# A cross-attention kernel with prompt tokens: first inner products in chunks, loads by order of use, last key chunk computed with the values

## The chip, the cores and the metric

The kernel runs on one core of a Trainium2 chip. The metric is the device time of one execution in microseconds. A core has TensorE (PE; its weight loads are shown as PEld), VectorE (DVE), ScalarE (ACT), GpSimd (POOL) and SyncE (SP, which here only issues transfers). Each engine runs its own instructions in order and waits for the others by semaphores; transfers (DMA) are issued by an engine and run beside it.

## What is computed

Eight batches (B). In each, 112 rows of x (S) attend with 20 heads of 16 channels (C = 320) to 371 text tokens and 4 prompt tokens, all rows of `ctx` (375 x 512). Everything is float32. Cut to what matters:

```python
q   = heads(x @ W_q)
k_t = heads(text @ W_k);  v_t = heads(text @ W_v)
probs_t  = softmax(q k_t^T / 4)
text_out = probs_t v_t
qsem = l2norm(probs_t @ text)              # 512 wide, per head and row
sem  = qsem @ l2norm(ip)^T                 # 4 numbers per head and row
fused = q k_ip^T / 4 + 0.5 * sem
ip_out = (softmax(fused) * spatial_mask) v_ip
out = (text_out + ip_out) @ W_out + b_out + x
```

The kernel never forms `qsem`. Its norm and its products with the prompts come from inner products of the context rows with each other: with G = ctx ctx^T, the squared norm of `p @ text` is p G p^T, and the products with the prompts are p times the last columns of G. G is symmetric, so only its upper triangle is computed, off-diagonal parts doubled ("first inner products" in the title are G for batch 0).

## The kernel before, in words

**For each batch** the context is loaded (`load_ctx`), transposed on TensorE (`transposed_context`, L339) into `ctxT` (512 channels as 4 chunks of 128 partitions, by tokens), and three products are made from it, each in three chunks of four matmuls (over the 4 channel chunks):

- `gram` (L362): G in three row chunks of 128 tokens, with 375, 247 and 119 columns. ACT doubles each out of PSUM into `ug` (L370), POOL halves the diagonal blocks (L371). `gram_to_dram` writes `ug` to a DRAM buffer `ud`, and `gram_to_groups` reads it back (L383) into `u`, once for each of four bands of 32 partitions, with token index modulo 32 on the partition.
- `values` (L409): 320 columns, in three token chunks, copied by ACT into `vext` (L416), written to DRAM (`vd`, L420) and read back by bands into `vr` (L429). `placed` (L445, POOL) copies the 16 value columns of the heads at hand from `vr` into the end of each region of `u`.
- `keys` (L393): the channels in chunks of 128, 371 token columns each. The third chunk has only 64 real columns (320 = 2 x 128 + 64), which `spread` has put apart with zeros between, so that each head lies in its band of 32 partitions. ACT copies each to `kT` (L400).

**The main loop** goes over batches and, in each, five groups of four heads (`steps`). `multiplied(b, g)` (L523) runs 48 products of 32-token blocks of probabilities with `u`: one pass gives p G, the text output, the softmax sum and the prompt products. In it, the scores (L476) and probabilities (L489 on DVE, L493 on ACT) of the step two ahead are made; SP carries the probabilities to `xg` (L496) and DVE transposes them in blocks (L504). `reduced` then takes the four PSUM banks of the step (ACT L536, DVE L538).

**The work for the next batch** is placed after the steps of the batch at hand, by `between`: after group 0 the inner products, after group 1 two chunks of values, after group 2 the third chunk of values and the first of keys, after group 3 the other two of keys, after group 4 the transposed context of the batch after it, and, in batches 1, 3 and 5, the queries of the next pair of batches (`project_queries`, L281 to L301). `finish` (softmax over prompts, sums, output projection) of the batch before is placed there too: its transposes (L620) after group 3, its output product (L633) after group 4, and the copy that empties that bank (L640).

**The order** of instructions on TensorE, SP and DVE is the order of the program text (a manual schedule), and of ACT and POOL too until the main loop. SP's transfers share eight semaphores in turn: each issue waits until the transfer eight before it has landed. So the order in which SP issues, and what an issue waits for, decides what stands behind it. ACT's queue issues a few transfers of the beginning.

PSUM has eight banks: four for `qd` (`ps_qd`), two for scores (`ps_sc`), two for everything else (`ps_mm`). `bank(name)` takes one of the last, `bank(name, spare=True)` one of the scores'.

**The beginning** (L700 to L742), before the loop: prompts normalised, context 0 transposed, its inner products, values, queries, keys, with the first scores between the key chunks; then context 1, the prompt projections (L237), and the first `placed`. SP's order there: context 0, W_v, W_k, the three writes of `ud`, W_k_ip, context 1, the twelve loads of `u`, the four of `vr`, then the probabilities of the first two steps. ACT's: the prompt rows, x of batch 0, W_q, and later `vd`.

## Time and profile before

| | us |
|---|---|
| median of 3 runs (497.8 to 499.25) | 498.68 |
| the profiled execution | 498.01 |
| its span, from first to last instruction | 496.2 |
| main loop starts (first L523) | 44.20 |
| last batch starts (first L523 of batch 7) | 437.13 |
| keys L393, 24 instructions of a batch (batches 1 to 7) | 7.67 |
| values L409, 24 instructions of a batch | 6.85 |
| inner products L362, 24 instructions: batch 0, and a later batch | 7.91, 5.27 |
| DMA: 61075 packets, 67.24 MB, mean rate | 136 GB/s |

One page shows one execution. Busy times are by engine; "the chain" is the work that ended last, followed back from the end, so a piece of work in it has its length in the time. Rows of the timeline give start, duration, engine, line, operation, tiles and sizes, and in brackets how long the engine had been idle and what ended that. `PE` matmuls overlap, so a row's own duration is longer than its share of the chain.

### The profile page before, as it was taken

The page shows a single profiled execution, that of the slowest core. Times are in us where ns is not written, and L with a number is a line of the kernel's source. Part 1 is how long each engine was busy: PE and PEld are TensorE (multiplying, and loading weights), DVE is VectorE, ACT ScalarE, POOL GpSimd, SP SyncE. Part 2 cuts the span into 40 slices and gives each one's busy share as a digit, 9 for nine tenths or more (in the row PEclk, how much of TensorE's full clock was granted, in tenths as well). Part 3 has the DMA queues.
Part 4 walks back from the last instruction along what each step waited for, and adds up shares of the span by engine and source line. Part 5 has one row for each costly group of instructions (what it writes and reads, how often), then busy time and mean ns, then how long its engine had stood idle before and what let it go on. Part 6 is the DMA issues. An engine that isn't in the chain of part 4 may idle for free.

```text
span 496.2 us, 12853 instructions
## 1 busy us (share of the span) xinstructions
PE 468.3 (94%) x5106; PEld 361.8 (73%) x5106; DVE 321.1 (65%) x692; ACT 180.1 (36%) x505; POOL 105.9 (21%) x245
## 2 busy tenths in 40 slices
PE   6999999999999999999999999999999999987963
PEld 3657777788777787788778787788777887766751
DVE  3045456687765775687756776687756776678862
ACT  2253232235334352335324342335324432243232
POOL 4301200002501124012501124012501232011540
PEclk9997999999999999999999999999999999998895
DMA  7588447542595236942595236842595227732300
GB/s 217 157 198 237 100 152 163 156 114 63 154 228 153 58 95 172 210 121 67 163 229 142 67 98 171 199 116 76 171 220 140 67 87 162 195 101 78 101 13 12
DMA packets 61075, 67.24 MB, mean 136 GB/s; under 512 B 22128, under 2 KB 56192, under 8 KB 61016
## 3 DMA queue, kind: packets, MB, share of 16 engines
q1 hardware_dynamic: 60096, 65.32, 50.3%
q10 hardware_dynamic: 920, 1.11, 0.8%
q8 instruction: 40, 0.66, 0.6%
q14 instruction: 19, 0.16, 0.1%
HBM read 31.65 MB, written 8.17 MB: 80 GB/s over the span
## 4 chain that ended last, share of the span: by engine, by line
PE 84%; DVE 5%; ACT 3%; DMA 2%; POOL 2%; issue 2%; SPq 1%; POOLq 0%; ACTq 0%; DVEq 0%
PE ps_qd L523 37%; PE ps_k L393 11%; PE ps_v L409 11%; PE ps_g L362 9%; PE ps_s L476 7%; PE ps_q L289 2%; PE ps_c L339 2%; PE ps_o L633 2%; DVE junk L538 1%; POOL wv L606 1%; DMA vr<-vd 1%; DVE qm L298 1%; PE ps_kip L237 1%; PE ps_ip L456 1%; DMA ip_sb<-in_ctx_dram 1%
## 5 line engine op out<-in xcount | busy, mean ns | idle before, releaser
L523 PE MATMUL ps_qd<-u,xgT 32*112 32x296 f32 (+11 forms) x3840 | 244.4, 365 | 3.5 <-POOL u L445 1.4
L523 PEld LDWEIGHTS ps_qd<-u,xgT 32*112 32x112 f32 x3840 | 196.8, 174 | 33.6 <-issue 7.3
L493 ACT ACTIVATE p<-ps_s,nmx 112x371 f32<-112x371 f32 x160 | 82.3, 568 | 159.8 <-DVE nmx L489 141.6
L489 DVE TENSOR_REDUCE nmx<-ps_s 112x1 f32<-112x371 f32 x160 | 77.4, 528 | 76.0 <-PE ps_s L476 74.7
L504 DVE STREAM_TRANSPOSE xgT<-xg 128x1536 f32<-128x1536 f32 x40 | 118.9, 2971 | 5.2 <-DMA xg<-p 5.2
L538 DVE CUSTOM_DVE_ANT_0 junk<-ps_qd,p 112x371 f32<-112x371 f32 x160 | 87.1, 544 | 45.3 <-ACT pvs L536 28.0
L476 PE MATMUL ps_s<-kT,qm 32*112 32x371 f32 x320 | 75.0, 496 | 2.8 <-ACT p L493 2.2
L445 POOL COPY u<-vr 128x64 f32<-128x64 f32 x120 | 26.6, 238 | 224.8 <-PE ps_qd L523 161.5
L393 PE MATMUL ps_k<-ctxT,wk_sb 128*128 128x371 f32 x192 | 63.6, 480 | 0.0
L409 PE MATMUL ps_v<-wv_sb,ctxT 128*128 128x320 f32 x192 | 55.6, 440 | 0.0
L393 PEld LDWEIGHTS ps_k<-ctxT,wk_sb 128*128 128x128 f32 x192 | 35.7, 190 | 21.7 <-issue 1.1
L476 PEld LDWEIGHTS ps_s<-kT,qm 32*112 32x112 f32 x320 | 36.8, 173 | 15.8 <-ACT kT L400 3.2
L362 PE MATMUL ps_g<-ctxT 128*128 128x375 f32 (+2 forms) x192 | 45.3, 394 | 0.7 <-issue 0.7
L409 PEld LDWEIGHTS ps_v<-wv_sb,ctxT 128*128 128x128 f32 x192 | 35.2, 190 | 13.5
L362 PEld LDWEIGHTS ps_g<-ctxT 128*128 128x128 f32 x192 | 33.4, 197 | 12.3 <-issue 3.8
L400 ACT COPY kT<-ps_k 128x371 f32<-128x371 f32 x24 | 11.3, 469 | 41.4 <-PE ps_k L393 41.3
L606 POOL TENSOR_TENSOR wv<-vip,w 112x1280 f32<-112x1280 f32 (+1 forms) x8 | 19.2, 2404 | 31.8 <-DVE w L604 31.8
L298 DVE TENSOR_SCALAR qm<-ps_q,emask 128x224 f32<-128x224 f32 (+1 forms) x25 | 9.2, 400 | 24.2 <-PE ps_q L289 24.0
L416 ACT COPY vext<-ps_v 128x320 f32<-128x320 f32 x24 | 10.2, 427 | 33.5 <-PE ps_v L409 33.5
L371 POOL TENSOR_TENSOR ug<-ug,half 128x128 f32<-128x128 f32 (+1 forms) x24 | 11.3, 472 | 41.6 <-ACT ug L370 41.6
L536 ACT COPY pvs<-ps_qd 112x21 f32<-112x21 f32 x160 | 16.5, 200 | 6.9 <-PE ps_qd L523 6.9
L289 PE MATMUL ps_q<-xT,wq_sb 128*128 128x224 f32 (+1 forms) x90 | 16.8, 332 | 1.9 <-ACT xT L284 0.9
(95 smaller groups left out, 272.4 us busy)
## 6 DMA issues: line engine op xcount, KB each, us to landing
xg<-p SPq DMA_DIRECT2D x160, 162.3 KB
u<-ud SPq DMA_DIRECT2D x32, 188.0 KB
vip<-vipd SPq DMA_DIRECT2D x8, 560.0 KB
ct<-in_ctx_dram SPq DMA_DIRECT2D x16, 256.0 KB
u<-ud SPq DMA_DIRECT2D x32, 124.0 KB
vr<-vd SPq DMA_DIRECT2D x32, 120.0 KB
vd<-vext SPq DMA_DIRECT2D x7, 480.0 KB
ud<-ug SPq DMA_DIRECT2D x7, 372.0 KB
```

Of the source, the lines that this page charges most:

```text
L289: nc.tensor.matmul(ps[:, : n * S], wq_sb[:, j, i * P : (i + 1) * P], xT[:, j, : n * S], start=(j == 0), stop=(j == NC - 1),)
L362: nc.tensor.matmul(ps[:, : T - t0], ctxT[:, e, t0 : t0 + P], ctxT[:, e, t0:T], start=(e == 0), stop=(e == NE - 1),)
L393: nc.tensor.matmul(ps[:, :TT], wk_sb[:, e, i * P : (i + 1) * P], s["ctxT"][:, e, :TT], start=(e == 0), stop=(e == NE - 1),)
L409: nc.tensor.matmul(ps[:, :C], ctxT[:, e, c * P : (c + 1) * P], wv_sb[:, e, :], start=(e == 0), stop=(e == NE - 1),)
L445: nc.gpsimd.tensor_copy(region(b, c)[:, :, UV - c * P :], s["vr"][:, c * QN : (c + 1) * QN, g, :])
L476: nc.tensor.matmul(ps[:S, :TT], qm[a * RG : (a + 1) * RG, i, r, j * S : (j + 1) * S], s["kT"][a * RG : (a + 1) * RG, i, :], start=True, st ...
L489: nc.vector.tensor_reduce(nmx, ps[:S, :TT], AX.X, ALU.max, negate=True)
L493: nc.scalar.activation(p, ps[:S, :TT], AF.Exp, bias=nmx)
L504: nc.vector.transpose(xT.rearrange("p j (k q) -> p q j k", q=QN), xg.rearrange("p q (j k) -> p q j k", k=RG),)
L523: nc.tensor.matmul(banks[a][:S, j * RG : UW], xT[a * RG : (a + 1) * RG, j, :S], region(b, c)[a * RG : (a + 1) * RG, q, q * RG :], start=(j ...
L538: nc.vector.tensor_tensor_reduce(out=junk, in0=ps[:S, :TT], in1=s["p", g][:, a, :], scale=1.0, scalar=0.0, op0=ALU.mult, op1=ALU.add, accu ...
L606: eng.tensor_tensor(wv, s["vip"][:, :, part], w.rearrange("p h n -> p n h").unsqueeze(3).to_broadcast([S, NIP, n, D]), ALU.mult,)
```

## The change

Five things, in the order of the diff. (1) The inner products of batch 0 are computed by column chunks: when token chunk c of the context is transposed, the blocks (r, c) with r up to c are multiplied, into three banks kept open (`first_gram`); 24 matmuls of 128 (or 119) columns stand in place of 12 of 375, 247 and 119. Between the pieces stand the transposes of the prompts. `awake(n)` issues n matmuls of the identity with itself into a spare bank that nobody reads, eight before the first context transposes and four after them. (2) `ud` becomes three DRAM buffers with rows as `u` holds them, value columns included (zeros), so that a band is read back by 32 rows of 1568, 1056 or 544 numbers each instead of 128 shorter ones; the writes are three per batch instead of one. (3) In batches 1 to 7 the third key chunk isn't computed by itself: its 64 columns of W_k are appended to W_v, the value matmuls have 384 columns, POOL copies the key columns into `k3` (token by spread channel, with zeros that are set once), and three transposes bring them into `kT`. (4) x and W_q move from ACT's queue to SP's, between W_v and W_k; in the beginning the loads of `u` and `vr` stand ahead of context 1 and W_k_ip. (5) The small tiles of `finish` have one buffer instead of two, and the bank of its transposes is one of the scores' in batches 0 to 6.

```diff
+    wv_sb = const.tile([P, NE, C + REST], F32, tag="wv_sb", name="wv_sb")
...
-    nc.scalar.dma_start(x_sb[:, 0, :], x[0])
-    load_channels(nc.scalar, wq_sb, w_q)
...
     load_embed(nc.sync, wv_in, w_v)
+    nc.sync.dma_start(x_sb[:, 0, :], x[0])
+    load_channels(nc.sync, wq_sb, w_q)
     load_embed(nc.sync, wk_sb, w_k)
...
+        s["ud"] = [dram.tile([RG, QN, WC[c]], F32, tag=f"ud{c}", name=f"ud_{b}_{c}") for c in range(NT)]
+        s["vext"] = work.tile([P, NT, C + REST], F32, tag="vext", name=f"vext_{b}", bufs=1)
...
+    def awake(n):
+        ps = bank(f"ps_w_{n}", spare=True)
+        for _ in range(n):
+            nc.tensor.matmul(ps[:, :P], ident, ident, start=True, stop=True)
+
+    def first_gram():
+        ctxT = st[0]["ctxT"]
+        banks = []
+        for c in range(NT):
+            banks.append(ps_qd.tile([P, 512], F32, tag="qd", name=f"ps_g_0_{c}"))
+            if c == NT - 1:
+                nc.gpsimd.tensor_copy(ctxT[:, :, TT:T], ipnT[:, :, :NIP])
+            c0, c1 = c * P, min(c * P + P, T)
+            for r in range(c + 1):
+                for e in range(NE):
+                    nc.tensor.matmul(
+                        banks[r][:, c0 - r * P : c1 - r * P],
+                        ctxT[:, e, r * P : (r + 1) * P],
+                        ctxT[:, e, c0:c1],
+                        start=(e == 0), stop=(e == NE - 1),
+                    )
+            yield
+        for c in range(NT):
+            doubled(banks[c], c)
+            yield
...
     def gram_to_dram(b, c0=0, c1=NT):
-        cols = slice(GCOL[c0], GCOL[c1])
-        nc.sync.dma_start(st[b]["ud"][:, cols], ug[:, cols])
+        for c in range(c0, c1):
+            nc.sync.dma_start(
+                st[b]["ud"][c].rearrange("i q w -> q i w"), ug[:, GCOL[c] : GCOL[c + 1]]
+            )
...
-                    region(b, c)[a * RG : (a + 1) * RG, :, : UV - c * P],
-                    s["ud"][:, GCOL[c] : GCOL[c + 1]].rearrange("(q i) t -> i q t", i=RG),
+                    s["u"][a * RG : (a + 1) * RG, OFF[c] : OFF[c] + QN * WC[c]],
+                    s["ud"][c].rearrange("i q w -> i (q w)"),
...
+            if b > 0 and i == FULL:
+                for c in range(NT):
+                    rows = min(P, TT - c * P)
+                    nc.tensor.transpose(
+                        ps[:, c * P : c * P + rows],
+                        s["k3"][:rows, c].rearrange("p a r d -> p (a r d)"),
+                        ident[:rows, :rows],
+                    )
+                nc.scalar.copy(s["kT"][:, i, :], ps[:, :TT])
+                yield
+                return
...
+        w = C if b == 0 else C + REST
...
+            if b > 0 and c == NT - 1:
+                nc.gpsimd.tensor_copy(
+                    s["k3"][:, :, :, 0, :],
+                    vext[:, :, C:].rearrange("p c (a d) -> p c a d", d=D),
+                )
...
-        ps = bank(f"ps_a_{b}_{h0}")
+        ps = bank(f"ps_a_{b}_{h0}", spare=b < B - 1)
...
     prompts = normalised_prompts()
     context = transposed_context(0)
-    products = gram(0)
+    products = first_gram()
+    next(prompts)
+    awake(8)
+    next(context)
+    awake(4)
+    next(context)
+    next(products)
     next(prompts)
     next(context)
-    next(context)
-    next(prompts)
-    next(context)
+    next(products)
+    next(products)
     order_values()
     for c in range(NT):
         next(products)
         gram_to_dram(0, c, c + 1)
     drain(values(0))
+    gram_to_groups(0, range(NT))
     values_to_dram(0, nc.scalar)
+    values_to_groups(0, nc.sync)
+    loaded[1] = load_ctx(1)
     load_embed(nc.sync, wkip_sb, w_k_ip)
     spread(nc.gpsimd, wq_sb)
+    nc.gpsimd.tensor_copy(wv_sb[:, :, C:], wk_sb[:, :, FULL * P : C])
     spread(nc.gpsimd, wk_sb)
     drain(project_queries(pairs[0]))
-    loaded[1] = load_ctx(1)
     run(("k", 0), lambda: keys(0))
-    gram_to_groups(0, range(NT))
-    values_to_groups(0, nc.sync)
```

`doubled` is the doubling and halving that stood in `gram` (L369 to L371).

## The prediction

> **What bounds the kernel now.** I read the page first (busy shares and the chain that ended last), then the chain in order of time for one batch, then the timeline of the first 45 us and of the places where one batch passes to the next, then the DMA packet records there.
>
> ```profile
> PE 468.3 (94%) x5106; PEld 361.8 (73%) x5106; DVE 321.1 (65%) x692; ACT 180.1 (36%) x505; POOL 105.9 (21%) x245
> ...
> PE 84%; DVE 5%; ACT 3%; DMA 2%; POOL 2%; issue 2%; SPq 1%; POOLq 0%; ACTq 0%; DVEq 0%
> ```
>
> The chain in order of time (start, us, what), one batch:
>
> ```profile
> 123.24 4.50 PE ps_v L409 x16
> 134.11 2.35 PE ps_v L409 x8
> 144.81 5.18 PE ps_k L393 x16
> 156.14 1.42 PE ps_c L339 x12
> ```
>
> TensorE is the bound in the steady part: it is busy 94% and carries 84% of the chain, and the projections of the next batch (values L409, keys L393) stand in the chain with their whole length. Time taken off them there is time off the end, as long as nothing else becomes late. A float32 matmul shows as two instructions, so x8 is one chunk of four matmuls.
>
> The beginning, first in busy times by stretch (TensorE with its number of instructions first, the granted clock third from the end), then in the timeline:
>
> ```profile
> 13.00:14.00 1.00, 1.00 (x3) 0.66 (x2) 0.00 (x0) 0.00 (x0) 0.00 (x0) 1.00 0.00 0
> 15.00:16.00 1.00, 1.00 (x6) 0.93 (x5) 0.00 (x0) 0.03 (x1) 0.46 (x1) 1.00 0.00 0
> ```
>
> ```profile
> 9.17 7.91 PE L362 MATMUL ps_g<-ctxT 128*128 128x375 f32 x24 [0.68 <-issue]
> ...
> 35.15 7.29 SPq L496 DMA_DIRECT2D xg<-p  x8
> ...
> 41.20 2.91 DVE L504 STREAM_TRANSPOSE xgT<-xg 128x1536 f32<-128x1536 f32 x1 [3.97 <-DMA xg<-p]
> ...
> 44.20 1.65 PE L523 MATMUL ps_qd<-u,xgT 32*112 32x392 f32 x6 [0.79 <-issue]
> ```
>
> The first inner products L362 take 7.91 us here and 5.27 us in each later batch. Weight loads of the 375-wide ones are 0.625 us apart until 14.3 us, though the clock column says 1.00: 375 columns in half of that would be the later pace, so TensorE ran at half speed until about 14.2 us, some 5.0 us after these matmuls began. From 9.17 to 43.4 us TensorE has work nearly throughout. The main loop then starts at 44.2 us, when L504 has ended, and L504 waited for the probabilities' transfer, issued only at 35.15 because SP was still at the loads before it.
>
> The timeline where batch 0 passes to 1, 1 to 2, 2 to 3 and 6 to 7:
>
> ```profile
> 103.60 0.59 POOL L445 COPY u<-vr 128x64 f32<-128x64 f32 x3 [6.12 <-DMA vr<-vd]
> ...
> 158.38 0.59 POOL L445 COPY u<-vr 128x64 f32<-128x64 f32 x3 [8.05 <-DMA vr<-vd]
> ...
> 215.53 0.59 POOL L445 COPY u<-vr 128x64 f32<-128x64 f32 x3 [7.32 <-DMA vr<-vd]
> 217.59 0.48 DVE L640 TENSOR_TENSOR ob<-ps_o,xb 112x320 f32<-112x320 f32 x1
> ...
> 436.84 0.59 POOL L445 COPY u<-vr 128x64 f32<-128x64 f32 x3 [13.32 <-DMA vr<-vd]
> 437.13 1.66 PE L523 MATMUL ps_qd<-u,xgT 32*112 32x392 f32 x7 [0.25 <-POOL u L445]
> ```
>
> At each change of batch the values of the next one come back through DRAM (vd, then vr) and POOL places them (L445) just before TensorE needs them. This is the second limit.
>
> **Keys behind the values (7 of 8 batches).** Removed: the third key chunk, 8 instructions at 5.18/16 = 0.324 us, 2.59 us. Added: 24 value instructions of 384 columns instead of 320. One of 320 costs (4.50+2.35)/24 = 0.285 us, one of 371 (keys) 0.324; by proportion 384 costs 0.335 to 0.342, so 0.050 to 0.057 more, 24 of them 1.2 to 1.4; I take 1.28. Three transposes at 1.42/12 = 0.118 are 0.36. Net 0.95 us off TensorE per batch, 6.65 for seven. Beside it: a POOL copy of 128x192 into k3, between the 128x64 copy (0.24 us) and the 112x320 product (0.87 us); it follows the third value chunk one whole step (about 11 us) before the transposes read it, so it costs nothing. ACT's three value copies grow by a fifth of 0.43 us; ACT is busy 36%. The bank of ps_a changes pool, since two banks would now be asked for in quick succession: its copy L624 comes after two key copies of 0.47, at about 4.15 us after the step's last matmul, and the second score wants that bank at about 4.3; no cost, up to 0.2 us a batch if that cover fails.
>
> But the gain is not spread evenly. The step between the fourth and fifth group of heads gets 2.59-0.36 = 2.24 us shorter, and the value route starts before that (vd waits for transfers issued after the fourth group's scores) and doesn't shorten with it. Room, from the end of the first of the three L445 copies to when the first matmuls could be late: where new queries are projected at the change (batches 1-2, 3-4, 5-6) it is 164.07-158.62 = 5.4 us, enough. At the other four something else ends last now. At 0-1 the fourth score bank is freed by L538, so that the scores start at 106.71 after 0.75 us of matmuls; against the copy's end at 103.84 the room is 2.1. At 2-3 L640 frees a bank at 218.07, and the second score stands 1.05 after the first matmul: 217.02-215.77 = 1.25. At 4-5 and 6-7 the same rows give 0.87 and 0.43. The shift of 2.24 exceeds them by 0.1, 1.0, 1.4 and 1.8 us, 4.3 in all, unless the route itself gets faster.
>
> **Inner products by way of DRAM.** The loads L383 go from 512 packets per chunk (1504, 992 or 480 bytes; 106, 76 and 37 ns each in the packet records) to 128 of 6272, 4224 and 2176. Such packets aren't in the trace; near ones are 2048 bytes at 107 and 5120 at 283 ns. By these rates (14 to 19 bytes per ns) one batch's loads take 16 engines 5.3 to 7.2 us against 7.0 now. Issues cost the same per transfer (0.49 us apart; 0.34 for the smallest one seen), the writes become three instead of one, +0.96 us of SP, which waits 137.5 us for L493 anyway. Since vd is queued behind these loads, the route gains 0 to 1.0 us; I take 0.4, nearer the issue rows than the packets. Excess then 0, 0.6, 1.0, 1.4 = 3.0. Steady part: 6.65-3.0 = 3.65 (2.35 with no help, 5.5 with 1.0).
>
> **The beginning.** Added: 12 matmuls on the identity, 24 instructions. The third kip group (L237), all cold, took 1.7 us for 8: 0.21 each, 0.11 in the warm ones. Eight matmuls from 1.4 us (identity ready at 1.30) end at 4.9; before, TensorE idled until 3.69, so the first transposes are 1.2 us late. Then 4 transposes (cold 0.26, warm 0.12), 4 matmuls, 4 transposes, one chunk product (8 instructions), 8 prompt transposes, 4 transposes, 16 and 24 instructions. Chunking adds no columns; the 119-wide products ran 0.88 us for 8, 0.11 each, so 48 cost 5.3 us warm, as the 24 wide ones. Warm from 6.4 (1.4 plus the 5.0 of above) the last ends at 14.2, against 17.08; warm from 4.4 at 13.0; and if the transposes break the run, so that the 5.0 count only from the second product at 12.6, at 19.4. I take 14.2, because the matmuls here fill at least two thirds of any 3.5 us from 1.4 on, while before the change the 3.5 us up to 11 us held 1.8 us of them and weren't enough.
>
> The Trainium skill, "TensorE: Matmul & The Clock Gate", Part 1, says that half speed ends after one busy window of about 3.4 us; by it warm would come at 4.8 to 8.2 and the products would end at 13.4 to 15.3. Part 4 of that page speaks against the change: transposes don't count as busy, by which the run of matmuls could be broken. The rows agree that 12 transposes from 3.69 on released nothing; none here shows a mixed run.
>
> TensorE's work up to the main loop would so end at 43.42-2.9 = 40.5 us. The probabilities' route: SP now goes ud, u, vr, context 1, wip, xg. ud starts at about 15.5 as now (all three products end together), u's packets at about 18.9 and run 5.6 us, stretched by vd to 26 (now 24.0 to 34.3); vr waits for vd (landed about 25.5) and holds SP for it with the context, wip and xg queued behind; packets of vr to 29.7, context 1 (2.7 us) to 32.2, wip (3.3) to 35.3, both before TensorE wants them (35.0 is met, wip at 37.0 after 1.0 of POOL's L120). First xg issue has its data at 30.1, but its packets go after wip: four take 3.7 (now 36.76 to 40.6), L504 starts at 39.4 and ends at 42.3, main loop at 42.2 to 42.4. So 2.0 us of the beginning are gained, not 2.9+0.79. Ends: -1.6 (products at 19.4) and +3.7 (TensorE alone decides). The half speed that the trace shows from 41.7 to 48.7 I leave as it is: the same little-used stretch stands before it.
>
> **Sum.** 3.65+2.0 = 5.65 us off the profiled execution's 498.01 (span 496.2 and 1.8 around it): 492.4. The median of the runs is 498.68, 0.67 above that one; against it 493.0.
>
> **Rivals.** *Nothing else binds:* vr arrives early enough and xg is not held by the queue: 6.65+3.7, 488.4. For it: POOL and DMA are half idle over a batch. Against: the row at 437.13 already waits. *Only the steady part, and little of it:* the route gets no faster and xg's queue eats the beginning: 2.35, 496.3. For it: the transfer records from 16.4 to 44.5 us are nearly without a gap. *It doesn't wake:* products end at 19.4, the main loop starts 1.6 later: 498.68+1.6-3.65 = 496.6. *Slower: the larger packets are slow.* 32 rows into 32 partitions at, say, 10 bytes per ns take 10.0 us a batch against 7.0; xg, vd and vr stand behind them in one queue, so each of the four tight changes loses about 2.8 more: 493.0+11 = 504. It decides from 1.7 us a batch on, 11.5 bytes per ns; no row is that slow for packets over 1 KB.
>
> **How the numbers follow.** Forecast 0.45 (own range 491 to 495), nothing binds 0.22, little of the steady part 0.16, no waking 0.08, slow packets 0.09. The range reaches into the second and third: 488.5 to 497. A measurement tells 0.3%, 1.5 us. Slower by that: the slow packets, 0.09. Within: the upper part of the third and fourth, 0.09. Faster: 0.82.
>
> **What would show it.** Right: values about 8.1 us a batch, no key row longer than 2.6; first products over by about 14 us with six or more instructions a us from 7 us on; L504 at 39 to 40; at 2-3, 4-5 and 6-7 TensorE waiting for L445. Wrong: the products at three a us beyond 12 us; L504 later than 41; packets of 6272 bytes above 550 ns; or waits of TensorE inside a step, where I found none.

## The result and the profile after

The changed kernel takes 506.08 us (median of 4 runs, 505.43 to 506.63) against 498.24 for the kernel before beside it: a ratio of 1.0155, 95% interval 1.0121 to 1.0189. The forecast was 493.0 with a range of 488.5 to 497, so it is slower where I said faster. The profiled execution took 505.55 us, its span is 503.8 (before 498.01 and 496.2).

The page of the changed kernel, busy times and the shares of the chain that ended last:

```profile
PE 468.9 (93%) x5119; PEld 363.4 (72%) x5119; DVE 321.0 (64%) x692; ACT 180.3 (36%) x505; POOL 109.8 (22%) x257
...
PE 65%; DMA 12%; DVE 7%; issue 5%; ACT 4%; SPq 3%; POOL 2%; POOLq 0%; DVEq 0%; ACTq 0%
```

TensorE's share of the chain fell from 84% to 65% and DMA's rose from 2% to 12%. TensorE is as busy as before, but its work no longer decides alone: transfers do. (A busy time can't show this, since TensorE that runs at half clock or slowly counts as busy.)

The timeline of the beginning (start, duration, engine, line, operation; in brackets the idle time before and what ended it):

```profile
1.36 3.78 PE L363 MATMUL ps_w<-ident 128*128 128x128 f32 x16 [1.36 <-POOL ident masks.py:199]
...
9.57 4.63 PE L376 MATMUL ps_g<-ctxT 128*128 128x128 f32 x40
...
40.64 0.71 POOL L121 COPY wip<-wip 128x64 f32<-128x64 f32 x3 [15.27 <-DMA wip<-in_L_xattn_W_k_ip_dram]
40.65 5.30 PE L243 MATMUL ps_kip<-ipT,wip 128*128 128x32 f32 x24 [3.82 <-DMA wip<-in_L_xattn_W_k_ip_dram]
...
43.78 2.89 DVE L565 STREAM_TRANSPOSE xgT<-xg 128x1536 f32<-128x1536 f32 x1 [9.38 <-DMA xg<-p]
...
46.78 1.01 PE L584 MATMUL ps_qd<-u,xgT 32*112 32x392 f32 x4 [0.82 <-issue]
```

The prompt products before the change:

```profile
39.82 3.60 PE L237 MATMUL ps_kip<-ipT,wip 128*128 128x32 f32 x24 [0.17 <-ACT ctxT L349]
```

The first products end at 14.2 us, as forecast (before: 17.08), and from there the gain is lost: TensorE waits 3.82 us for W_k_ip, the prompt products then run at half clock (5.30 us, before 3.60), the block transpose waits for the probabilities until 43.78, and the loop starts at 46.78, before 44.20. The block transpose decides: it ends at 46.7, the prompt products at 45.95.

I cut the span in four at fixed places of the program: the first product of the main loop, the first of batch 7, the last of batch 7, the end.

| us | before | after | difference |
|---|---|---|---|
| main loop starts | 44.20 | 46.78 | +2.58 |
| from there to batch 7 | 392.93 | 394.65 | +1.72 |
| products of batch 7 | 40.04 | 41.80 | +1.76 |
| from there to the end | 19.05 | 20.53 | +1.48 |
| span | 496.2 | 503.8 | +7.5 |

The second row hides several large parts. The steps that carry the projections got 0.89 us a batch shorter (the step after the fourth group -2.17, those with the values +0.85 and +0.43), 6.2 us in seven batches. The seven changes of batch gave back 5.7: 4.2 at the four without new queries, 1.5 at the three with them. The late transfers there delayed DVE in the following step (+1.03 in batch 1, +1.41 in batch 3).

Batch 7 is longer because its clock was at half for longer: 11.9 us of it, before 6.8. A window early in it (TensorE busy first, with its number of instructions, granted clock third from the end), of before and then of after:

```profile
440.00:447.00 7.00, 5.96 (x105) 4.62 (x101) 5.85 (x11) 3.45 (x9) 0.71 (x3) 1.00 0.35 93
```

```profile
440.00:447.00 7.00, 6.52 (x43) 4.63 (x45) 4.44 (x10) 1.03 (x2) 1.45 (x4) 0.53 0.35 96
```

At 0.53 of the clock TensorE's rows show 43 instructions in the 7 us instead of 105; 1.4 us of the window stand before the batch starts at 441.43. The clock fell at 439.70 us, behind the first of two waits at the change to batch 7:

```profile
438.52 2.42 PE L694 MATMUL ps_o<-wo_sb,aT 128*112 128x320 f32 x6 [1.50 <-ACT p L554]
441.43 1.97 PE L584 MATMUL ps_qd<-u,xgT 32*112 32x392 f32 x8 [0.48 <-POOL u L506]
```

The first (before: 0.53 us) was for ACT, behind a block transpose of DVE that had itself waited 0.94 us for the probabilities; the second was for the values of `vr`.

### The profile page after: what moved, and what is told of

Its sections match the earlier page's. It is cut to its first block, busy times and chain, and to the rows that moved or that the text cites. A ratio compares the mean times of both kernels' runs of the same rounds, so it can differ in the third digit from the quotient of the medians.

```text
span 503.8 us, 12927 instructions
## 1 busy us (share of the span) xinstructions
PE 468.9 (93%) x5119; PEld 363.4 (72%) x5119; DVE 321.0 (64%) x692; ACT 180.3 (36%) x505; POOL 109.8 (22%) x257
## 4 chain that ended last, share of the span: by engine, by line
PE 65%; DMA 12%; DVE 7%; issue 5%; ACT 4%; SPq 3%; POOL 2%; POOLq 0%; DVEq 0%; ACTq 0%
PE ps_qd L584 27%; PE ps_v L465 13%; PE ps_s L537 5%; PE ps_g L405 5%; DMA xg<-p 5%; PE ps_k L448 5%; DMA vd<-vext 4%; DVE junk L599 2%; PE ps_q L295 2%; DMA wip<-in_L_xattn_W_k_ip_dram 2%; ACT p L554 2%; DMA vr<-vd 1%; PE ps_o L694 1%; DVE nmx L550 1%; PE ps_c L346 1%
## 5 line engine op out<-in xcount | busy, mean ns | idle before, releaser
L584 PE MATMUL ps_qd<-u,xgT 32*112 32x104 f32 (+11 forms) x3840 | 245.7, 367 | 6.0 <-POOL u L506 4.2
L584 PEld LDWEIGHTS ps_qd<-u,xgT 32*112 32x112 f32 x3840 | 202.3, 175 | 35.4 <-POOL u L506 7.5
L565 DVE STREAM_TRANSPOSE xgT<-xg 128x1536 f32<-128x1536 f32 x40 | 118.5, 2963 | 19.4 <-DMA xg<-p 19.4
L506 POOL COPY u<-vr 128x64 f32<-128x64 f32 x120 | 27.4, 238 | 221.3 <-PE ps_qd L584 146.9
L465 PE MATMUL ps_v<-wv_sb,ctxT 128*128 128x384 f32 (+1 forms) x192 | 64.6, 487 | 0.0
L448 PE MATMUL ps_k<-ctxT,wk_sb 128*128 128x371 f32 x136 | 46.1, 482 | 0.0
L405 PE MATMUL ps_g<-ctxT 128*128 128x375 f32 (+2 forms) x168 | 37.4, 379 | 0.0
L448 PEld LDWEIGHTS ps_k<-ctxT,wk_sb 128*128 128x128 f32 x136 | 25.0, 190 | 15.7 <-issue 1.1
L405 PEld LDWEIGHTS ps_g<-ctxT 128*128 128x128 f32 x168 | 28.1, 190 | 8.8 <-issue 0.5
L472 ACT COPY vext<-ps_v 128x384 f32<-128x384 f32 (+1 forms) x24 | 11.3, 473 | 42.2 <-PE ps_v L465 32.3
L694 PE MATMUL ps_o<-wo_sb,aT 128*112 128x320 f32 x48 | 17.5, 503 | 2.3 <-ACT p L554 1.5
L597 ACT COPY pvs<-ps_qd 112x21 f32<-112x21 f32 x160 | 16.5, 200 | 6.5 <-PE ps_qd L584 6.5
```

Of the source, the lines that this page charges most:

```text
L405: nc.tensor.matmul(ps[:, : T - t0], ctxT[:, e, t0 : t0 + P], ctxT[:, e, t0:T], start=(e == 0), stop=(e == NE - 1),)
L448: nc.tensor.matmul(ps[:, :TT], wk_sb[:, e, i * P : (i + 1) * P], s["ctxT"][:, e, :TT], start=(e == 0), stop=(e == NE - 1),)
L465: nc.tensor.matmul(ps[:, :w], ctxT[:, e, c * P : (c + 1) * P], wv_sb[:, e, :w], start=(e == 0), stop=(e == NE - 1),)
L506: nc.gpsimd.tensor_copy(region(b, c)[:, :, UV - c * P :], s["vr"][:, c * QN : (c + 1) * QN, g, :])
L565: nc.vector.transpose(xT.rearrange("p j (k q) -> p q j k", q=QN), xg.rearrange("p q (j k) -> p q j k", k=RG),)
L584: nc.tensor.matmul(banks[a][:S, j * RG : UW], xT[a * RG : (a + 1) * RG, j, :S], region(b, c)[a * RG : (a + 1) * RG, q, q * RG :], start=(j ...
```

## The experiments

Sixteen kernels ran. In each call the kernel before ran on the same chip; its median was 497.4 to 498.5, and the ratios are against it. All compute the whole reference. The table gathers them; the three columns on the right are us from each kernel's profiled execution, cut as above (the tail is given in the text where it matters).

| kernel | median | ratio, interval | loop starts | to batch 7 | batch 7 |
|---|---|---|---|---|---|
| e1_loads_first | 501.30 | 1.0038 to 1.0169 | 43.91 | 394.98 | 40.47 |
| e2_keys_alone | 505.73 | 1.0136 to 1.0219 | 48.23 | 394.02 | 41.02 |
| e3_two_buffers | 503.02 | 1.0077 to 1.0184 | 45.39 | 394.89 | 41.40 |
| e4_early_vd | 504.56 | 1.0092 to 1.0186 | 45.81 | 396.29 | 40.62 |
| e5_early_u | 515.98 | 1.0307 to 1.0365 | 47.08 | 403.43 | 40.40 |
| e6_early_u_vd | 518.29 | 1.0351 to 1.0406 | 47.40 | 410.95 | 40.03 |
| e7_old_packets | 498.99 | 0.9985 to 1.0033 | 42.91 | 394.57 | 40.52 |
| e8_fold_alone | 497.49 | 0.9970 to 1.0026 | 43.17 | 392.42 | 40.59 |
| e9_write_spread | 506.76 | 1.0134 to 1.0237 | 45.38 | 396.78 | 42.94 |
| e10_vd_first | 491.75 | 0.9837 to 0.9938 | 44.87 | 386.98 | 39.17 |
| e11_all_mended | 490.19 | 0.9794 to 0.9886 | 40.52 | 387.25 | 41.65 |
| e12_context_late | 491.11 | 0.9818 to 0.9923 | 42.35 | 387.24 | 40.53 |
| e13_vd_first_alone | 498.15 | 0.9974 to 1.0035 | 44.25 | 392.70 | 40.45 |
| e14_large_packets | 495.63 | 0.9925 to 0.9984 | 44.39 | 389.57 | 40.46 |
| e15_first_as_before | 491.45 | 0.9824 to 0.9905 | 44.02 | 387.79 | 39.27 |
| e16_writes_cut | 491.64 | 0.9822 to 0.9902 | 40.76 | 388.38 | 42.97 |

The three columns come from one execution each, and two of them scatter. The changed kernel and e2 to e6 have the same beginning, and their loops start anywhere from 45.39 to 48.23; the kernel before, e8, e10 and e13 have nearly the same, and theirs start from 43.17 to 44.87. The start follows the moment at which the clock first goes to full: 4.81 to 7.58 us in the first six, with the loop 39.8 to 40.9 us after it; 13.43 to 14.93 us in the other four, with the loop 29.6 to 29.9 us after it. So a loop start that differs by less than 2 or 3 us from another's says little by itself. Batch 7 runs at half clock for 3.4 us (e10) to 13.9 us (e9) and takes 39.2 to 43.0. The middle column is steadier: 386.98 to 387.79 in e10, e11, e12 and e15, which all have the old layout, the fold and `vd` early; where the route is late it is 394.65 to 394.98 in the changed kernel, e1 and e3, but 396.78 in e9, whose order there is the same.

### First round: one part of the change at a time

**e1_loads_first**: in the beginning W_k_ip and context 1 stand ahead of the loads of `u` again.

```diff
+    load_embed(nc.sync, wkip_sb, w_k_ip)
+    loaded[1] = load_ctx(1)
     gram_to_groups(0, range(NT))
     values_to_dram(0, nc.scalar)
     values_to_groups(0, nc.sync)
-    loaded[1] = load_ctx(1)
-    load_embed(nc.sync, wkip_sb, w_k_ip)
```

> The changed kernel, with W_k_ip and context 1 loaded ahead of the loads of u and vr in the beginning (the order from before the change); nothing else differs. Theory (late transfers): in the changed kernel the main loop starts at 46.78 us because W_k_ip lands at 40.6, behind vr, which waits for vd. With it ahead, the prompt projections start when TensorE reaches them (36.8 us) and the loop at 41 to 42.5: 4.5 us less, 501.6 us. Rival (larger packets are slow and hold the rest): the loads of u take as long as now wherever they stand, the loop waits for u and xg instead: 505 to 507 us. Rival (added engine work): nothing moves, 506 us.

The loop starts at 43.91, 2.9 us earlier than in the changed kernel and 1.5 earlier than the earliest of the six with its beginning, and the time is 501.3: the order in the queue is a part of the loss. The time is as expected, but the loop did not reach the 41 to 42.5 that was to give it. It is still 3.4 us later than the best start seen (e11, 40.5), and the time no better than before.

**e2_keys_alone**: the fold undone (the conditions `b > 0` become `b > B`, the values have 320 columns).

> The changed kernel with the third key chunk computed by itself in every batch and 320 value columns, as before the change; the rest is kept. Theory (late transfers): the steps after the fourth group get 2.2 us longer, those after the second and third 1.3 shorter, and the waits at the change of batch disappear, with what follows from them in batches 1, 3 and 7: some 3.5 us less, 502.6 us, with the loop still starting at 46.8. Rival (added engine work is nothing, the fold is a gain that is lost elsewhere): 6.2 us more, 512 us.

505.73, no slower than with the fold within the interval, though it has 6.2 us more projections: from the loop's start to batch 7 it takes 394.02 against 394.65. In the changed kernel the fold is worth nothing. The theory's 502.6 did not come either: the waits at the changes of batch went with the fold, and they and what follows them were worth about as much as the fold, not 3.5 us more.

**e3_two_buffers**: `ex` in `finish` has two buffers again.

```diff
-            return small.tile([S, H, NIP], F32, tag=name, name=f"{name}_{b}_{h0}", bufs=1)[:, :n]
+            bufs = 2 if name == "ex" else 1
+            return small.tile([S, H, NIP], F32, tag=name, name=f"{name}_{b}_{h0}", bufs=bufs)[:, :n]
```

> The changed kernel with two buffers for the one small tile ex of finish, so that ACT's load of the exponential's table at the end needn't wait for DVE. Theory: the last 20.5 us (from the last L584 to the end) get 1.3 us shorter, as before the change: 504.8 us. Rival: the end is longer because TensorE runs at half speed there; then the end stays within 0.3 us, 506 us.

The tail went from 20.53 to 19.28. ACT's timeline, of the changed kernel and of this one:

```profile
482.38 1.28 ACT L656 ACT_TABLE_LOAD   x1 [1.84 <-DVE fu L654]
483.68 0.26 ACT L656 ACTIVATE ex<-fu 112x64 f32<-112x64 f32 x1
```

```profile
479.02 1.28 ACT L657 ACT_TABLE_LOAD   x1
480.81 0.26 ACT L657 ACTIVATE ex<-fu 112x64 f32<-112x64 f32 x1 [0.50 <-DVE fu L655]
```

With one buffer the load of the exponential's table, which stands ahead of the activation, waits 1.84 us for DVE, and its 1.28 us come after the wait. With two buffers the load doesn't wait, and its 1.28 us lie inside the activation's wait. My reading, which the rows don't show by themselves, is that with one buffer there are two things to wait for (the input, and the release of the output) and that one of the two waits falls to the load.

**e4_early_vd**: `vd` is issued behind the work of group 2, a step earlier than in the changed kernel, ahead of the next probabilities.

> The changed kernel with the write of vd issued right after the third chunk of values (after the third group) and not after the u loads that follow the fourth; same transfers otherwise. Theory (the way of the values through DRAM, 17.5 us from the start of the fourth group to the first L506 of the next batch, is what ends last at the changes of batch): vr can be issued about 3 us earlier, the waits there go (5.7 us over seven changes), and so do the late xg after them (2.4) and half speed in batch 7 (1.7): 9.8 us less, 496.3 us; at least 494.5, at most 500. Rival (added engine work) and rival (larger packets): within 1 us of 506.

This expectation failed by 8 us. The late steps of batches 1 and 3 went (1.0 and 1.4 us) and the change to batch 7 lost 0.7 less, but batch 1 to 2 lost 3.1 us more and others 0.2 to 0.6: the probabilities now stood behind `vd`, and at 1 to 2 a block transpose waited 1.89 us for them, in the changed kernel 0.39.

### Second round: is it the loads, their packets or the fold

**e5_early_u**: the loads of `u`, chunks 0 and 1, one step earlier (after the work of group 1), chunk 2 after group 2. **e6_early_u_vd**: `vd` early as well.

> The changed kernel with the loads of the next batch's u one step earlier: chunks 0 and 1 behind the work of group 1, chunk 2 behind the products of group 2; vd and vr as they were. Theory: in the changed kernel u, vd, the prompt values and the probabilities of two steps all stand in the 17.5 us from group 3 to the change of batch, the DMA engines are full, and vr comes too late once the keys are shorter. Then the waits at the changes of batch (+5.74 against before), the late probabilities behind them (+2.44 in group 1 of batches 1 and 3) and the cold clock of batch 7 (+1.77) go, and 506.1 becomes 496 to 498. Rival, the waits come from something that this leaves in place (vd or vr by themselves, or engine work): 504.5 to 506.5. Rival, the early loads only take the room of the probabilities of groups 3 and 4: these steps grow by over 0.5 us each and the time is 501 to 505.

> As the kernel before it, and the write of vd is issued behind the work of group 2 instead of behind the products of group 3. Theory (full DMA engines): the room that the early u leaves lets vd go without harm to the probabilities, so it is as fast as the kernel with u alone or up to 1 us faster, 495 to 498. Rival, vd early does harm by itself, as it may have when the vd write alone was moved (504.56): slower than the kernel with u alone by 2 us or more.

Both theories fell. For e5 the second rival was right in kind and too small; e6 is 2.3 us slower than e5, as its rival said. SP's timeline and a block transpose of e5:

```profile
192.18 9.10 SPq L426 DMA_DIRECT2D u<-ud  x8
201.38 3.62 SPq L557 DMA_DIRECT2D xg<-p  x4
```

```profile
207.85 2.95 DVE L565 STREAM_TRANSPOSE xgT<-xg 128x1536 f32<-128x1536 f32 x1 [3.55 <-DMA xg<-p]
```

Eight issues hold SP for 9.1 us instead of 5.1 in the changed kernel, since each must wait until the transfer eight before has landed, and those are now the writes of `ud` and the context. The probabilities are queued behind, and DVE waits 3.55 us for them. Issuing earlier doesn't make a route earlier if the queue blocks on it.

**e7_old_packets**: the layout of `ud`, its write and the loads of `u` as before the change; all else changed.

> The changed kernel with ud and the loads of u as they were before the change: rows of the token, packets of 1504, 992 and 480 bytes; the rest stays changed. Theory that the large packets are a cause of the late vr: the changes of batch lose 2 us or more of their 5.74, 502.5 or less with a loop that starts at the same place. Rival, the packets don't matter (6.6 against 7.2 us of the sixteen engines per batch): 505 to 507, since the loads take a little longer.

498.99 against 506.08: nearly all of the loss goes with the layout, that is with the write, the loads or both. The time is inside the theory's, but not in its place: it looked for the gain at the changes of batch, with the same loop start, and the part between is the same (394.57). Most of it is in the beginning (42.91, where the forecast had 42.2 to 42.4; 45.39 at best with the changed layout), the rest in batch 7, which has 6.8 us of half clock instead of 11.9. The share of the 16 DMA engines that is busy, in tenths, in slices of 0.2 us from 13 to 21 us, of the changed kernel and of this one:

```profile
DMA  0300000002231023122222222222222297989999
```

```profile
DMA  0040000069910792820098589999999999999999
```

The write of `ud`'s chunk 0 (196 KB) in the changed kernel runs at 2 tenths, some four engines, and its 128 packets last from 14.75 to 17.97 although each takes 96 ns on average; the old write of 188 KB runs at 6 to 9 tenths and is over in 0.9 us. The three writes end at 20.41 instead of 16.52, and the loads of `u` wait for them.

The Trainium skill states this rule: "DMA: Bandwidth & Descriptors", "Why a DMA increments its semaphore by 16 and not by 1" and again "Rules for kernel authors", says that the number of engines is the largest up to 16 that divides the slowest dimension of both access patterns. Here the write's DRAM side is `i q w -> q i w`, with 4 bands outermost: four engines by the rule, and 128 x 96 ns over 3.22 us is 3.8 by the records.

**e8_fold_alone**: the kernel before with the fold and what it needs in room, nothing else.

> The kernel before the change with nothing but the third key chunk behind the values (and what it needs in room: one buffer for the small tiles of finish except ex, the bank of its transposes among the scores'). Theory that the route of u, vd and vr has no slack whatever its packets are: projections -6.2, changes of batch and the steps behind them +5 to +6, so 497 to 498.5, the same as before within 0.3%. Rival, that the large packets are what makes the route late: 493.5 to 495.5, the gain of 3.65 that was predicted for the steady part, or more.

497.49 against 498.48, ratio 0.9998: the same. So the fold alone gives nothing with the old packets either, as the first theory said.

### Third round: the route

Here is where the fold's gain goes, at the change from batch 6 to 7, in SP's, POOL's and TensorE's rows of e8 (the first row of TensorE is the start of group 4's products, the last the start of batch 7):

```profile
425.33 1.95 SPq L387 DMA_DIRECT2D u<-ud  x4
427.33 0.43 SPq L442 DMA_DIRECT2D vd<-vext  x1
430.17 2.88 SPq L451 DMA_DIRECT2D vr<-vd  x4
...
435.30 0.59 POOL L467 COPY u<-vr 128x64 f32<-128x64 f32 x3 [12.60 <-DMA vr<-vd]
...
425.56 1.03 PE L545 MATMUL ps_qd<-u,xgT 32*112 32x392 f32 x7
435.59 1.24 PE L545 MATMUL ps_qd<-u,xgT 32*112 32x392 f32 x8 [1.75 <-POOL u L467]
```

It is one chain: `vd` issued, landed, `vr` issued, landed, placed, first product. From the start of group 3 `vd` is issued after 10.1 to 10.9 us and the next batch starts after 18.6 to 19.7, where no queries are projected. Before the change the chain was as long (placed after 17.6 to 19.6 us), and the fold makes TensorE's own work beside it 2.17 us shorter.

**e10_vd_first**: e8 with `vd` ahead of the four loads of chunk 2 of `u`, still behind that step's probabilities. **e13_vd_first_alone**: the same swap in the kernel before.

```diff
+                values_to_dram(b + 1, nc.sync)
                 gram_to_groups(b + 1, (2,))
-                values_to_dram(b + 1, nc.sync)
```

> The kernel before with the key fold alone, and the write of vd issued ahead of the four loads of u's third chunk instead of behind them (about 2 us earlier on SP, 8.2 instead of 10.15 us from the start of group 3, and still behind the probabilities of that step). Theory: at the changes of batch without queries the next product waits for the chain vd issued, landed, vr issued, landed, placed, which is as long with the fold as without (17.4 to 19.4 us), so that the fold's 2.17 us in group 3 are lost there; two us earlier, the chain is shorter than TensorE's own work, and the time is 493 to 495.5. Rival, the loads of u's third chunk or the probabilities are then late instead (as when vd was moved a step ahead): 497 or more.

> The kernel before the change with vd issued ahead of u's third chunk and nothing else. Theory that this only sets the fold's gain free: without the fold, TensorE's own work was 0.3 to 1.2 us longer than the chain at the changes of batch, so there is nothing to gain, and the time is that of before within 1 us (steady part 392 to 393 us from the start of the loop to batch 7). Rival, vd late costs the kernel before too: 2 us or more faster than before.

```profile
422.51 0.53 SPq L442 DMA_DIRECT2D vd<-vext  x1
423.10 2.42 SPq L387 DMA_DIRECT2D u<-ud  x4
426.07 1.84 SPq L451 DMA_DIRECT2D vr<-vd  x4
...
431.56 0.59 POOL L467 COPY u<-vr 128x64 f32<-128x64 f32 x3 [11.35 <-DMA vr<-vd]
...
423.07 1.04 PE L545 MATMUL ps_qd<-u,xgT 32*112 32x392 f32 x7
431.85 1.43 PE L545 MATMUL ps_qd<-u,xgT 32*112 32x392 f32 x7 [0.49 <-POOL u L467]
```

In e10 `vd` is issued 0.56 us before group 4's products instead of 1.77 behind them, and batch 7 starts 8.78 us after them instead of 10.03. The four cases make a square: neither 498.07 (the kernel before, in e13's call), swap alone 498.15, fold alone 497.49, both 491.75. Neither part gains by itself; together they gain 5.6 us on the kernel before in the same call (497.38). From the loop's start to batch 7, e13 takes 392.70 and e10 386.98, 5.7 less, near the 6.2 that the projections lost. That settles where the gain had gone.

**e9_write_spread**: the changed kernel, in the beginning each write of `ud` cut into four of 32 rows.

```diff
+    def first_to_dram(c, eng, qs):
+        for q in qs:
+            eng.dma_start(
+                st[0]["ud"][c][:, q, :], ug[q * RG : (q + 1) * RG, GCOL[c] : GCOL[c + 1]]
+            )
...
-        gram_to_dram(0, c, c + 1)
+        first_to_dram(c, nc.sync, (0, 1))
+    for c in range(NT):
+        first_to_dram(c, nc.scalar, (2, 3))
```

> The changed kernel; only in the beginning each of the three writes of ud is cut into four transfers of 32 rows (two issued by SP, two by ACT), with the same layout in DRAM and the same large loads behind them. Theory: with the bands as the outermost of the write's three dimensions its 128 packets of 1568 bytes go to about four engines (94 ns each, yet 3.2 us for all, 14.75 to 17.97; the kernel with the old layout takes 0.9 us); all of u, vr, context 1 and W_k_ip stands behind it. Cut up, the writes end by 17.5 instead of 20.4, W_k_ip lands some 3 us earlier, the main loop starts at 43 to 44.5 instead of 45.4 to 48.2, and the time is 502.5 to 504. Rival, the large loads themselves are what is late in the beginning: the loop starts at 45.5 or later and the time is 505 to 507.

Missed: the writes end at 17.74 instead of 20.41, but the loop starts at 45.38 and the time is 506.76, which are the rival's numbers. W_k_ip is still last of the loads there and its packets stand between those of the probabilities for 4.7 us (33.0 to 37.7; in the changed kernel 6.2, in e7 3.0). With that order the write explains only a part of the late start, and in the time the cut is worth nothing; what slows W_k_ip there I can't say.

**e11_all_mended**: the changed kernel with the old packets, e1's order, e3's buffers and `vd` first. **e12_context_late**: as e11, but context 1 loaded behind the probabilities of group 0.

> The changed kernel with four things mended at once: the packets of ud and u as before the change, W_k_ip and context 1 ahead of the loads of u in the beginning, two buffers for ex, and vd ahead of u's third chunk. By the sizes measured one by one: the fold alone with vd first, less the earlier start of the loop (42.9 instead of 44.2 in the kernel before): 491.5 to 494. Rival, that the order in the beginning only moves the wait to the probabilities (first block transpose at 40.9 whatever the order): 494 to 496.

> As the kernel with the four things mended, but context 1 is loaded behind the probabilities of group 0 and transposed behind the prompt projections. Theory that the beginning is bound by the bytes that the DMA engines must move before the first block transpose: 0.77 MB fewer stand ahead of it, it starts 2 to 4 us earlier than with context 1 ahead, and the time is 1 to 3 us lower than that of the kernel before it here. Rival, that TensorE then waits for context 1 before the loop, or the probabilities are made no earlier: same or up to 2 us slower.

e11 is the fastest of all, 490.19, 1.6% (1.1 to 2.1%) below before; the loop starts at 40.52, 3.7 us earlier. In e12 the first block transpose comes no earlier (37.38 against 37.49), as its rival said. The loop starts later, at 42.35, since TensorE stands 2.29 us among the transposes of context 1, for a bank that ACT empties only when DVE is done with that block transpose. The page of e11 shows the chain back in TensorE's hands:

```profile
PE 465.5 (95%) x5119; PEld 360.6 (74%) x5119; DVE 321.6 (66%) x692; ACT 180.3 (37%) x505; POOL 109.7 (22%) x254
...
PE 83%; DVE 6%; ACT 3%; DMA 3%; issue 3%; POOL 1%; SPq 0%; POOLq 0%; DVEq 0%; ACTq 0%
```

### Fourth round: what the packets and the first part are worth when nothing else is late

**e14_large_packets**: e11 with the changed kernel's `ud`, writes and loads. **e16_writes_cut**: e14 with the writes of chunks 0 and 1 cut into four, in every batch. **e15_first_as_before**: e11 with the first inner products in one piece and no products of the identity.

> The kernel with the four things mended, but with the changed kernel's layout of ud, its writes and its large loads. If the large packets cost only where the route had no room: steady part 387 to 388 us as with the old packets, the loop starting 2 to 3.5 us later (43 to 44 instead of 40.5, since the writes to four engines end 3.9 us later), and 492 to 494. Rival, the large packets cost in every batch: steady part above 390 us and 495 or more.

> The mended kernel with large packets, with the writes of ud's chunks 0 and 1 cut into four transfers of 32 rows each, in every batch (in batch 0 chunk 2 as well, half of them on ACT's queue). If the write is what costs: the first loads of u start 3 us earlier, the loop starts at 40.5 to 42 instead of 44.4, the steady part is 387 to 388.5 instead of 389.6, and the time is 490.5 to 493. Rival, the large loads cost by themselves: loop 43.5 or later, steady part 389 or more, 494.5 to 497.

> The kernel with the four things mended, but with the inner products of batch 0 as before the change, in one piece and without the products of the identity. Theory that the beginning is bound by what the DMA engines have to move: the first products end 2.9 us later and the loop starts 0 to 1.5 us later, 490 to 492. Rival, that the earlier products pass on in full: the loop starts 2.5 to 3 us later, 492.5 to 493.5.

e14 takes 495.63, 5.4 us more than e11: the time is its rival's, the steady part lies between the two expectations (the loop starts 3.9 us later and the part up to batch 7 is 2.3 us longer). Cutting the writes gives back 3.6 us of the first and 1.2 of the second, and the time is 491.64: loop, middle part and time as the theory of e16 had them. The DMA engines of e16 in the same slices as above:

```profile
DMA  3000002700187494743054047033249999999999
```

The writes of chunks 0 and 1 end at 17.39 instead of 19.83 in e14, and W_k_ip, which goes beside or behind them, takes 3.2 us (17.7 to 20.9) instead of 6.3 (17.3 to 23.6). The first packets of `u` don't come 3 us earlier as expected (22.7 against 21.6); the last are over at 30.8 instead of 33.9. The large loads themselves cost at most some 1.1 us more in the steady part, which is hardly beyond its scatter. So in this order the harm was in the write, and in the shape of its access pattern, not in the size of the packets. In batch 0 e16 also moves half of the writes to ACT's queue, and that was not tried by itself.

e15's loop starts 3.5 us later than e11's, as the rival said (the first products end 2.5 us later): by the profiled runs the earlier first products pass on in full. In the medians it is 1.3 us (491.45 against 490.19, intervals that overlap), inside the theory's 490 to 492, so a gain in the time is not shown clear of the scatter. In the profiled run batch 7 was 2.4 us shorter than e11's; its length goes from 39.2 to 43.0 over all these runs, mostly with the time at half clock, and I had no control of it.

## Why the prediction was wrong, step by step

**How far off.** The profiled run took 13.2 us more than the 492.4 that was forecast for it: 4.6 in the beginning (-2.0 forecast, +2.6 measured), 5.4 from the loop's start to batch 7 (-3.65 and +1.72), and 1.8 in batch 7 and 1.5 behind it, to which the sum gave nothing.

**Right.** The projections: 0.95 us a batch and 6.65 in all were forecast, 0.89 and 6.2 came. The waking: with the products of the identity full speed comes at 6.20 us (forecast 6.4) and the first products end at 14.2 (forecast 14.2). That the points were met so closely is luck: in the thirteen runs with these products full speed came between 4.81 and 7.58 us and the products ended between 13.5 and 14.9. The 5.0 us that the prediction counted from the first matmul are not a fixed time (3.4 to 6.2 here), but its wider figures, 4.8 to 8.2 and 13.4 to 15.3, hold in every one. The Trainium skill, "TensorE: Matmul & The Clock Gate", Part 4, spoke against it, since transposes between the matmuls don't count as busy in the same way; four of them stand among the products before 6.20, and no run had to wait longer than 7.58. The place of the second limit was right too: at the changes of batch without new queries TensorE waits for L506, as foreseen.

**The step that failed first** was in the part on the inner products by way of DRAM: "the writes become three instead of one, +0.96 us of SP". I priced the writes by their issue alone and gave their data no more time than the old write of 188 KB takes, 0.9 us. With the bands outermost they take 3.2, 1.9 and 1.3 us and end at 20.4 us, with the old layout (e7) at 16.5. Everything behind them in the queue came late: the loads of `u` were to run from about 18.9 to 26 and ran from 19.4 to 28.9, context 1 was to land by 32.2 and did by 34.8, W_k_ip by 35.3 and did by 39.5, and the transpose L504 (now L565) by 39.4 and came at 43.8. The term of -2.0 became +2.6. With the old packets the same order gives 42.91, and with W_k_ip ahead 40.5. That it is the write is shown where W_k_ip stands ahead: cutting it takes the loop's start from 44.39 to 40.76 and the time from 495.6 to 491.6 (e14, e16). In the changed kernel's own order the write is a part only, since there the cut left the time where it was (e9). A term of the paragraph on the beginning failed beside it: W_k_ip was to take 3.3 us with the probabilities behind it, and took 6.2, mixed with their packets, so that the first of their transfers landed only at 41.4. What stretched it, beyond the write, the runs don't show.

**The route** was to gain 0.4 us by the larger packets; it gained 0.2 (placed 18.8 us after the start of group 3 instead of 19.0, mean of seven). The loads take 6.7 us of the 16 engines a batch instead of 7.2, inside the bounds that I gave. So the loss at the four tight changes was mis-sized by the help that did not come: 3.0 forecast, 4.3 if the route stays, and 4.2 measured (0.2, 1.4, 0.9 and 1.8). With the fold alone (e8), whose route is the old one, moving `vd` set 4.8 us free there. The mechanism was right, and what I lacked was the scatter: issued 10.1 to 10.2 us after the start of group 3, `vd` lands between 13.0 and 15.1 us after it in one run (six changes). A wait that such a transfer ends costs its late cases and is not repaid by its early ones.

**Left out of the sum.** The changes with new queries, for which I found 5.4 us of room, lost 1.5 (e10 lost 0.35), and the step behind batches 1 and 3's first group 2.4: SP's next probabilities are queued behind `vr`, which waits for `vd`. These 3.9 us are the larger part of the 5.4 by which that stretch was missed; the tight changes are 1.2 of it. I followed `vd` to TensorE and not to what stands behind it on SP. The single buffer of `ex` cost 1.25 us of the 1.48 at the end, to which the sum gave no term. And batch 7 (+1.8) had 5.1 us more of half clock than before, which the sum did not foresee; it began behind a wait of TensorE, but e16 has 13.7 us of half clock that begin 14 us after batch 7 started, so the wait is not shown to be its cause.

**The rivals.** The time came out on the side of the slower rival and 2 us beyond its 504, but by another mechanism: it wanted loads at 10 bytes per ns, and the packets of 6272 bytes took 408 ns, 15.4 bytes per ns. It named the right place (the packets' new shape, with vd and vr behind them) and, by e14 and e16, the wrong transfer. At 0.09 it was given too little: I had searched the loads for a price and not the write, which the same edit had reshaped.

**What stays open:** why W_k_ip lands so late when it is last (e9), whether the layout's loads or its writes cost more in that order (e7 changes both), and what decides how long batch 7 runs at half clock.

## What to carry to other kernels

When an edit reshapes a transfer through DRAM, price both directions, and look at the outermost dimension of each access pattern before the size of the packets: here four bands outermost put a write on about four of the 16 DMA engines. When work is taken off the engine that bounds a loop, find the chain that runs beside it and shorten that first; here the swap of two lines in a queue was worth nothing alone and made the difference between 0 and 5.6 us for the fold. And of every transfer that comes late, ask who stands behind it in its queue, not only who waits for its data.

## What the runs showed of the hardware

The clock is granted in steps: in these traces it changes at multiples of 3.41 us after its last change (6.20, 40.34, 50.58, 439.70, 446.52 us in the changed kernel: 10, 3, 114 and 2 times 3.41 apart). When the first full speed comes differs from run to run, 4.81 to 7.58 us with the same beginning, and the start of the loop moves with it by up to 2.8 us (text under the table). In the changed kernel two stretches at half speed began during or right behind waits of TensorE (3.8 us in the beginning, 1.5 and 0.5 us at the change to batch 7) and lasted 10.2 and 6.8 us. That the waits caused them was not tried by itself, and something else must do it too: the kernel before runs at half speed from 41.7 to 48.6 us, where its prompt products had waited 0.17 us, and all eighteen traces have 3.4 us or more of it in batch 7. Large packets brought little: 6272 bytes go at 15.4 bytes per ns and engine, 1504 at 14.2.
